# Two-layer graph and mixture kernel: layer 1's full pages in doubles of 512 rows of one expert

## The chip, the cores and the metric

The kernel runs on one core of a Trainium2 chip. The metric is the device time of one execution in microseconds; the time before is the median of three runs, 1977.85 us (1976.66 to 1979.0).

## What is computed

The input is 128 graphs of 64 nodes with 256 features, 8192 tokens in all. Two layers follow each other; each has a graph convolution over the 64 nodes and then a mixture of experts. The change concerns only the mixture of the second layer (layer 1), cut to what matters:

```python
x_flat = x.reshape(-1, D_MODEL)                       # 8192 x 256
gate_logits = x_flat @ Wg + bg + bias                 # 8 experts
topk_vals, topk_idx = jax.lax.top_k(gate_logits, 2)
topk_w = jax.nn.softmax(topk_vals, axis=-1)
h = relu(einsum('td,edh->teh', x_flat, W1) + b1)      # 256 -> 512, per expert
y = einsum('teh,ehd->ted', h, W2) + b2                # 512 -> 256
out = einsum('ted,te->td', y, combine)                # the two chosen experts, weighted
```

The input of this mixture is the layer's normalized x, and its result is added to x.

## The kernel before

The kernel computes each expert only for its own tokens. While layer 1's graph stage runs over 32 blocks of 256 tokens, a router (class `Router`, the object `r1`) sends each token's row of 258 words (256 features, the token's number, and the difference of its two logits) into a table in DRAM, at the next free place of the expert: L408, an indirect DMA from GpSimd, twice for a token. An expert's rows lie together. Afterwards the experts' rows are worked through in **pages** of 256 rows. A remainder of at most 128 rows is a half page.

How many pages each expert has is known only at run time. `page_table` (L432) computes on VectorE, in some fifty small instructions, a list of pages (row in the table, expert) and a list of half pages, into the tile `tab`; `load` (L547) reads four entries at a time into registers. The program holds a fixed number of page bodies: `likely` pages and half pages always run, and a block under `tc.If` (L1602) holds further ones, for routings that need more. With this kernel's numbers 58 full and 7 half pages always run, and the conditional block doesn't.

Four **first pages**, numbered -4 to -1, are the first 256 rows of experts 0 to 3. They are found full after block 16 (`look`, L179), and are fetched while the graph stage still runs (`fetch_first`, L568); their work is spread over the end of that stage and the transition from it.

One page goes through these steps, each a helper:

- `fetch1` (L1169) on SyncE's queue loads the page's rows into `px` (six buffers), and `load1` (L1162) the expert's first matrix with its bias into `pw` (three buffers) and the second bias into `pb2` (four).
- `flip1` (L1188): TensorE turns the rows (four instructions of L89), ScalarE copies them to `pxT`.
- `up` (L1195): the first product on TensorE (L1206), with relu on ScalarE (L1209).
- `down` (L1212): the second product (L1220), with the expert's matrix in `fw2`, which is resident.
- `share` (L1224): the weight of the expert, from the difference of logits.
- `answer` (L1234): on VectorE bias (L1237) and weight (L1239) into `py_s` (three buffers), and then, for each tile of 128 rows, `add` (L423).
- `add` (L425) is an indirect DMA from GpSimd that adds 128 rows of 256 words to the output in DRAM, at the tokens' rows, which it reads from `px`. A token appears in a page once, so the two adds of a page are declared independent; an add of another page waits until both have landed. A `px` buffer is free when its adds have landed.

`run` (L1593) lines pages up: at each step the page two ahead is fetched, the present page is turned, the former page finished (`share`, `down`, `answer`), and the present one goes `up`. The order is written out by hand: pages in order, with five of the seven half pages put in at every eighth page and the last two at the end (L1598 to L1601). The order on TensorE, VectorE and ScalarE is the program's own. SyncE and GpSimd's queues are put in order by a scheduler. [...]

At the transition the order is: `page_table`; `share` and `answer` of page -4; `flip1(-2)`; `down(-3)`; `up(-2)`; `share` and `answer` of page -3; and then `run`, whose first steps fetch page -1 and page 0, turn page -1, finish page -2, and take page -1 `up`.

Of the kernel before, what the change touches and what calls it, by code (L numbers as in the profile page):

```python
# [19 lines left out]
P = 128  # L20
# [86 lines left out]
class Router:  # L107
# [15 lines left out]
    def __init__(self, tc, pool, small, dram, n, D, E, K, T, pg, S, epoch, name, R, likely, halves, total=None, like=None):  # L123
        nc = tc.nc
        self.tc, self.nc, self.pool, self.small = tc, nc, pool, small
        self.n, self.D, self.E, self.K, self.T, self.pg, self.S, self.name = n, D, E, K, T, pg, S, name
        self.epoch, self.EP, self.pitch = epoch, epoch * T * P, S + pg
        self.halves = halves
        self.pages = K * n // pg + (E // 2 if halves else E - 1)
        self.likely_pages, self.likely_halves = likely  # L130
        self.full_pages = -(-(K * n - E * (pg - 1)) // pg)
        self.chunks = E + (K * (n - 3 * T * P) + E * self.EP) // S if S < n else E
        self.J = (n - 1) // S + 1
        self.spare = self.chunks * self.pitch
        self.W = D + 2
        assert T == 2 and epoch == 4 and n % self.EP == 0 and S % pg == 0 and (5 * T * P <= S or S >= n)
        assert self.pages <= 4 * P and self.spare + pg < 2 ** 24
        if like is None:
            self.tri = pool.tile([P, P], BF16, name=name + "tri")
            self.ones = pool.tile([P, P], BF16, name=name + "ones")  # L140
            make_upper_triangular(nc, self.tri, diag=False)
            nc.gpsimd.memset(self.ones, 1.0)
        else:
            self.tri, self.ones = like.tri, like.ones
        self.R = R
        self.seen = None
        self.expert = self.iota([P, E], [[1, E]], 0, "expert")
        self.page = self.iota([P, 4], [[1, 4]], 4, "page")
        self.total, self.each = total, (1 if total is not None else K)
        self.dest = self.iota([P, T, K], [[P * self.each, T], [0 if self.each == 1 else 1, K]], self.each, "dest")  # L150
        self.base = pool.tile([P, E], F32, name=name + "base")
        nc.vector.tensor_scalar(self.base, self.expert, float(self.pitch), None, op0=ALU.mult)
        self.zero = pool.tile([P, 3 * E], F32, name=name + "zero")
        nc.gpsimd.memset(self.zero, 0.0)
        self.map = pool.tile([P, self.J, E], F32, name=name + "map")
        nc.gpsimd.memset(self.map, 0.0)
        nc.vector.tensor_copy(self.map[:, 0, :], self.base)
        if self.J > 1:
            self.nth = self.iota([P, self.J, E], [[1, self.J], [0, E]], 0, "nth")
            self.end, self.delta, self.alloc, self.none = (  # L160
                pool.tile([P, E], F32, name=name + x) for x in ("endrow", "delta", "alloc", "none"))
            self.used = pool.tile([P, 1], F32, name=name + "used")
            for t, v in ((self.delta, 0), (self.alloc, 1), (self.used, E), (self.none, 1)):
                nc.gpsimd.memset(t, float(v))
            nc.vector.tensor_scalar(self.end, self.base, float(S), None, op0=ALU.add)
        self.filler = pool.tile([P, pg // P, self.W], F32, name=name + "filler")
        nc.gpsimd.memset(self.filler, 0.0)
        fill_to = self.filler[:, :, D].bitcast(I32)
        if total is None:
            self.answer = dram.tile([n * K, D], F32, name=name + "y")  # L170
            nc.gpsimd.iota(fill_to, pattern=[[0, pg // P]], base=n * K, channel_multiplier=0)
        else:
            nc.gpsimd.iota(fill_to, pattern=[[P, pg // P]], base=n, channel_multiplier=1)
            nc.sync.dma_start(out=total[n:n + pg, :].rearrange("(t p) d -> p t d", p=P), in_=self.filler[:, :, :D])
        self.table = dram.tile([self.spare + pg, self.W], F32, name=name + "x")
        self.taken = None
        self.fill(nc.sync, self.spare)

    def look(self, m):  # L179
# [10 lines left out]
        v.memset(self.firsts, 0.0)  # L190
        v.tensor_scalar(self.firsts[:, :m], t, float(self.spare), None, op0=ALU.add)
        self.full_pages -= m

    def look_back(self):

# [227 lines left out]
    def add(self, i, x, y):  # L423

        i, d = f"{self.name}add{i}", self.nc.gpsimd.indirect_dma_start(  # L425
            out=self.total[:, :],
            out_offset=bass.IndirectOffsetOnAxis(ap=x[:, self.D:self.D + 1].bitcast(I32), axis=0),
            in_=y, in_offset=None, compute_op=ALU.add)
        self.tc.declare_no_dep(d.ins, group=i, reason="a page has a token once")
        self.tc.add_to_no_dep_group(i, d.ins)  # L430

    def page_table(self, scratch):  # L432
# [94 lines left out]
        if self.halves:  # L527
# [8 lines left out]
            v.tensor_scalar(self.tab[:, 2, :], row, float(self.spare), None, op0=ALU.add)  # L536
            v.tensor_scalar(self.tab[:, 3, :], exp, float(E - 1), None, op0=ALU.min)

    def fill_end(self, e):

        if e % 4 == 0:
# [28 lines left out]
        d = self.nc.sync.dma_start(out=out, in_=self.table[ds(row, self.pg), :].rearrange("(t p) d -> p t d", p=P))  # L570
        self.tc.declare_no_dep(d.ins, group=self.name + "late", reason="full pages get no rows")

    def fetch_half(self, row, out):

        n = self.pg // 2
        self.nc.sync.dma_start(out=out, in_=self.table[ds(row, n), :].rearrange("(t p) d -> p t d", p=min(n, P)))

    def fetch(self, i, row, out):
        d = self.nc.sync.dma_start(out=out, in_=self.table[ds(row, self.pg), :].rearrange("(t p) d -> p t d", p=P))
        if i < self.full_pages:  # L580
            self.tc.declare_no_dep(d.ins, group=self.name + "fill", reason="full pages have no filler rows")
            self.tc.add_to_no_dep_group(self.name + "full", d.ins)
# [11 lines left out]
def two_layer_gnn_moe_kernel(ctx: ExitStack, tc: tile.TileContext, a: dict, out: bass.AP):  # L594
# [107 lines left out]
    with tc.tile_pool(name="c0", bufs=1) as c0, \  # L702
# [196 lines left out]
        for _ in norm_b(0):  # L899
# [3 lines left out]

        r0 = Router(tc, const, small, dram, N, D, E0, K0, T, P, 14 * P, 4, "r0", 3, ((K0 * N // P - EARLY) // 4 * 4 + 4, E0 // 2 - 4), True)
        r1 = Router(tc, const, small, dram, N, D, E1, 2, T, 2 * P, N, 4, "r1", 1,
                    (N // P - E1 // 4 - FIRST, E1 - 1), True, total=out, like=r0)
        assert W == r0.W
        r0.begin(counts, work, route)
        H, R, Q, V, S, Y = (chain(blocks, f) for f in (choose, residual_a, square_sum, normalize, slots, scale))
# [133 lines left out]
    with tc.tile_pool(name="wx0", bufs=3, reuse_waits="tile") as wx, \  # L1043
# [21 lines left out]
        def fetch(j):  # L1065
            Q = pairs[j]
            Q["px"] = px = wx.tile([P, 2, W], F32, name="px", bufs=22)
            if j >= npair:
                regs["row"] = r0.load(2, 4 * (j - npair), ENG.SP)
                for i in range(4):  # L1070
                    q, h = i // 2, i % 2 * P // 2
                    r0.fetch_half(regs["row"][i], px[h:h + P // 2, q:q + 1, :])
                return
            for q in range(Q["n"]):
                i = 2 * j + q
# [72 lines left out]
    fw2 = keep.tile([P, E1, KF, D], F32, name="fw2")  # L1148
    wx = ctx.enter_context(tc.tile_pool(name="wx1", bufs=2, side="right", reuse_waits="tile"))
    PG = 2 * P  # L1150
    pages = {i: dict(n=2 if i < r1.pages else 1) for i in range(-FIRST, r1.pages + E1)}
    regs = {}

    likely = r1.likely_pages
    some = r1.pages + r1.likely_halves

    def listed(i):

        what, i = (2, i - r1.pages) if i >= r1.pages else (0, i)
        return what, i, i % 4 == 0 or i == (r1.likely_halves if what else likely)  # L1160

    def load1(i, e):  # L1162
        Q = pages[i]
        Q["w"] = w = wx.tile([P, F1W], F32, name="pw", bufs=3)
        nc.sync.dma_start(out=w, in_=fw1[ds(e, 1)].rearrange("o p f -> p (o f)"))
        Q["b2"] = b2 = wx.tile([P, D], F32, name="pb2", bufs=4)
        nc.sync.dma_start(out=b2, in_=a["L1_ffn_b2"][ds(e, 1), :].to_broadcast([P, D]))

    def fetch1(i):  # L1169
        Q = pages[i]  # L1170
        Q["x"] = x = wx.tile([P, 2, W], F32, name="px", bufs=6)
        if i < 0:
            if i == -FIRST:
                regs["first"] = r1.load_first(0, ENG.SP)
            r1.fetch_first(regs["first"][i + FIRST], x)
            load1(i, i + FIRST)
            return
        what, m, new = listed(i)
        if new:
            regs["row", what], regs["esp", what] = r1.load(what, m, ENG.SP), r1.load(what + 1, m, ENG.SP)  # L1180
        if what:
            r1.fetch_half(regs["row", what][m % 4], x[:, :1, :])
        else:
            r1.fetch(i, regs["row", what][m % 4], x)
        load1(i, regs["esp", what][m % 4])


# [46 lines left out]
    def answer(i):  # L1234
# [2 lines left out]
        nc.vector.tensor_add(y[:, :n, :], Q["py"][:, :n, :], Q["b2"].unsqueeze(1).to_broadcast([P, n, D]))  # L1237
        for t in range(n):
            nc.vector.tensor_scalar(y[:, t, :], y[:, t, :], p[:, t:t + 1], None, op0=ALU.mult)  # L1239
            r1.add(i, Q["x"][:, t, :], y[:, t, :])  # L1240

    with tc.tile_pool(name="c3", bufs=1, reuse_waits="tile") as c3, \
            tc.tile_pool(name="work3", bufs=2, reuse_waits="tile") as work, \
# [309 lines left out]
            (3, place1),  # L1553
            (4, load_w2),
        ))
        r1.page_table(work.tile([P, 512], F32, name="scratch", bufs=1))
        share(-4)
        answer(-4)
        flip1(-2)
# [6 lines left out]
    with tc.tile_pool(name="pt4", bufs=2, space=PSUM, reuse_waits="tile") as pt_pool, \  # L1566
# [7 lines left out]
        def finish(i):  # L1574
            if i >= 0:
                what, m, new = listed(i)
                if what == 0 and m < E1:
                    r1.fill_end(m)
                if new:
                    regs["e", what] = r1.load(what + 1, m, ENG.PE)  # L1580
            share(i)
            down(i, regs["e", what][m % 4] if i >= 0 else i + FIRST)
# [12 lines left out]
            staggered(len(order), [(lag, lambda n, f=f: f(order[n]))  # L1595
                                   for lag, f in ((-2, fetch), (0, then(flip1)), (1, finish), (0, then(up)))])

        order = list(range(-2, likely))  # L1598
        for i in range(r1.pages, some - 2):
            order.insert(order.index(E1 * (i - r1.pages + 2)), i)  # L1600
        run((*order, *range(some - 2, some)))  # L1601
        with tc.If(r1.needed(likely)):  # L1602
            run((*range(likely, r1.pages), *range(some, r1.pages + E1)))


# [30 lines left out]
```

## Time and profile before

| What | Value |
|---|---|
| Median of three runs | 1977.85 us |
| The profiled execution | 1981.85 us, span 1979.7 us |
| TensorE busy | 1852.6 us, 94% of the span |
| VectorE, ScalarE, GpSimd busy | 58%, 51%, 57% |
| Granted TensorE clock, mean | 0.972 |
| Adds to the output (L425) | 131, 1553 ns each, 203.4 us |
| Loads of matrices (L1165) | 69, 514 KB each |
| Loads of rows of full pages (L579, L570) | 62, 258 KB each |

Times are of one execution recorded by the hardware profiler. A group of instructions is named by its line, engine, operation and tiles; "idle before" is the time its engine stood still just ahead of it, and what follows the arrow ended that wait. A view in order of time gives start and duration in us, and the wait in square brackets. PE is TensorE, DVE VectorE, ACT ScalarE, POOL GpSimd, and SPq the DMA queue of SyncE; a line there is the issue of a transfer and not the transfer itself. The experts' pages of layer 1 fill the stretch from about 1475 us to the end.

### The profile page before, as it was taken

To read this page: it belongs to the slowest core of one execution; us is meant where nothing else is said; L and a number is where in the kernel's file an instruction comes from. 1 tells how busy PE (TensorE), PEld (TensorE's weight loads), DVE (VectorE), ACT (ScalarE), POOL (GpSimd) and SP (SyncE) were. 2 spreads that over 40 slices of the span, in tenths; PEclk is the share of its full clock that TensorE was granted. 3 is DMA by queue.
4 is the path that set the end of the run, shared out by engine and by line. 5 is a ranking of instruction groups with operands and counts; after the bars stand their busy time and mean duration, and the time that the engine had idled before them with its cause. 6 is when DMAs were issued, how large, how long until landed. Compare 5 with 4: busy or idle time off the path is not lost. (4 is left out here: it accounts for less than half of the span.)

```text
span 1979.7 us, 35753 instructions
## 1 busy us (share of the span) xinstructions
PE 1852.6 (94%) x9906; PEld 1611.9 (81%) x9906; DVE 1150.0 (58%) x4248; ACT 1001.9 (51%) x2047; POOL 1134.9 (57%) x1113
## 2 busy tenths in 40 slices
PE   7999999999956898999989899999999999999992
PEld 6888888888845777888877788888888888888882
DVE  5899999999975333344333479999952222222221
ACT  5888888888831222222222266666643333333331
POOL 1377777777677677777777634444444434444433
PEclk9999999999977999999999899999999999999996
DMA  4234555553377988766665799787338766666663
GB/s 128 70 128 141 162 165 163 161 165 130 126 249 231 298 260 259 217 205 208 211 206 177 297 337 336 270 271 268 123 116 197 174 149 163 159 162 164 161 158 62
DMA packets 260780, 377.37 MB, mean 191 GB/s; under 512 B 54216, under 2 KB 214616, under 8 KB 260576
## 3 DMA queue, kind: packets, MB, share of 16 engines
q1 hardware_dynamic: 183600, 228.63, 38.8%
q0 software_dynamic: 62736, 135.21, 22.4%
q10 hardware_dynamic: 14240, 11.12, 1.7%
q8 instruction: 90, 1.47, 0.3%
q14 instruction: 114, 0.93, 0.2%
HBM read 211.67 MB, written 165.50 MB: 191 GB/s over the span
## 5 line engine op out<-in xcount | busy, mean ns | idle before, releaser
L408 POOL DMA_INDIRECT r0x<-xs,r0row x384 | 386.4, 1006 | 216.3 <-ACT lat L810 113.7
L415 POOL DMA_INDIRECT r0y<-px x390 | 378.9, 972 | 123.1 <-DMA r0y<-px 50.0
L1115 PE MATMUL py<-lat,pxT 128*128 x1616 | 386.4, 383 | 19.3 <-ACT pxT L1089 15.9
L425 POOL DMA_INDIRECT out_x<-py_s,px x131 | 203.4, 1553 | 294.1 <-DMA out_x<-py_s,px 189.3
L1119 DVE TENSOR_SCALAR px<-py,px 128x256 f32<-128x256 f32 x390 | 170.8, 480 | 306.2 <-PE py L1115 301.5
L1115 PEld LDWEIGHTS py<-lat,pxT 128*128 128x128 f32 x1616 | 293.1, 191 | 60.2 <-ACT pxT L1089 21.8
L1089 ACT COPY pxT<-pt 128x512 f32<-128x512 f32 x188 | 109.7, 585 | 346.1 <-PE pt L1086 232.3
L1209 ACT ACTIVATE phid<-ph,pw 128x256 f32<-128x256 f32 (+1 forms) x264 | 122.0, 462 | 294.6 <-issue 146.9
L408 POOL DMA_INDIRECT r1x<-xs,r1row x128 | 136.1, 1063 | 184.2 <-ACT hn L1349 54.7
L821 PE MATMUL ps<-lat 128*128 128x256 f32 x1024 | 238.9, 382 | 0.0
L785 PE MATMUL ph<-lat 128*128 128x256 f32 x1024 | 232.5, 386 | 2.7 <-DVE lat L808 2.0
L1220 PE MATMUL py<-fw,phid 128*128 (+1 forms) x1016 | 230.7, 380 | 1.8 <-issue 1.0
L1206 PE MATMUL ph<-pxT,pw 128*128 128x256 f32 (+1 forms) x1056 | 227.2, 368 | 0.6 <-DMA pw<-in_L_ffn_W1b 0.6
L785 PEld LDWEIGHTS ph<-lat 128*128 128x128 f32 x1024 | 195.4, 193 | 29.4 <-issue 2.4
L821 PEld LDWEIGHTS ps<-lat 128*128 128x128 f32 x1024 | 193.5, 192 | 27.9
L1206 PEld LDWEIGHTS ph<-pxT,pw 128*128 128x128 f32 x1056 | 192.8, 190 | 26.0 <-issue 1.4
L1237 DVE TENSOR_TENSOR py_s<-py,pb 128x512 f32<-128x512 f32 (+1 forms) x67 | 44.5, 664 | 290.7 <-DMA out_x<-py_s,px 232.7
L1220 PEld LDWEIGHTS py<-fw,phid 128*128 128x128 f32 x1016 | 187.9, 190 | 25.3 <-issue 1.6
L1086 PE MATMUL pt<-ident,px 128*128 128x128 f32 x780 | 120.7, 276 | 10.5 <-DMA px<-r0x 10.3
L1086 PEld LDWEIGHTS pt<-ident,px 128*128 128x128 f32 x780 | 97.3, 142 | 35.1 <-issue 7.0
L808 DVE SCALAR_TENSOR_TENSOR lat<-ph,c_L_gnn_b,rms 128x256 f32<-128x256 f32 x256 | 111.9, 476 | 22.9 <-ACT rms L72 22.9
L788 ACT ACTIVATE lat<-ph,c_L_gnn_b 128x256 f32<-128x256 f32 x256 | 103.5, 470 | 32.6 <-PE ph L785 28.3
(353 smaller groups left out, 2882.7 us busy)
## 6 DMA issues: line engine op xcount, KB each, us to landing
y<-r0y SPq DMA_DIRECT2D x64, 768.0 KB
px<-r0x SPq DMA_DIRECT2D x376, 129.0 KB
pw<-in_L_ffn_W1b SPq DMA_DIRECT2D x69, 514.0 KB
x<-x SPq DMA_DIRECT2D x64, 256.0 KB
px<-r1x SPq DMA_DIRECT2D x62, 258.0 KB
pb<-in_L_ffn_b SPq DMA_DIRECT2D x69, 128.0 KB
r0x<-r0filler ACTq DMA_DIRECT2D x64, 129.0 KB
lat<-in_x SPq DMA_DIRECT2D x32, 256.0 KB
```

Source lines behind the costliest of these rows:

```text
L408: i = self.nc.gpsimd.indirect_dma_start(out=self.table[:, :], out_offset=bass.IndirectOffsetOnAxis(ap=row[:, t, k:k + 1], axis=0), in_=xs[ ...
L415: d = self.nc.gpsimd.indirect_dma_start(out=self.answer[:, :], out_offset=bass.IndirectOffsetOnAxis(ap=x[:, self.D:self.D + 1].bitcast(I32 ...
L425: i, d = f"{self.name}add{i}", self.nc.gpsimd.indirect_dma_start(out=self.total[:, :], out_offset=bass.IndirectOffsetOnAxis(ap=x[:, self.D ...
L785: nc.tensor.matmul(ph[:, c, :], lhsT=w1[:, k, ts(2 * j + c, P)], rhs=B["aggT"][:, k, :], start=(k == 0), stop=(k == KD - 1))
L808: nc.vector.scalar_tensor_tensor(hT[:, c, :], B["ph", c // 2][:, c % 2, :], b1[:, c:c + 1], B["rms"], op0=ALU.add, op1=ALU.mult)
L821: nc.tensor.matmul(B["po"][:, t, :], lhsT=B["hT"][:, c, ts(t, P)], rhs=w2[:, c, :], start=False, stop=(t == T - 1 and c == KH - 1))
L1086: nc.tensor.transpose(pt[:, k, ts(q, P)], Q["px"][:, q, ts(k, P)], ident)
L1115: nc.tensor.matmul(py[:, q, :], lhsT=xT[q][:, k, ts(h, P)] if parts == 2 else xT[:, k, ts(q, P)], rhs=lat[:, ds(e, 1), k, :].rearrange("p ...
L1119: nc.vector.tensor_scalar(px[:, q, :D], py[:, q, :], px[:, q, D + 1:D + 2], None, op0=ALU.mult)
L1206: nc.tensor.matmul(ph[c - c0][:, :m], lhsT=w[:, k * F1 + c * P:k * F1 + (c + 1) * P], rhs=Q["xT"][:, k, :m], start=(k == 0), stop=(k == KD ...
L1209: nc.scalar.activation(hid[:, c, :m], ph[c - c0][:, :m], AF.Relu, bias=w[:, KD * F1 + c:KD * F1 + c + 1], scale=1.0)
L1220: nc.tensor.matmul(py[:, t, :], lhsT=Q["hid"][:, c, ts(t, P)], rhs=fw2[:, ds(e, 1), c, :].rearrange("p o d -> p (o d)"), start=(c == 0), s ...
```

## The change

Full pages of one expert are taken in twos, a **double** of 512 rows: one load of rows into `px4` (three buffers), one load of the matrix and the bias, and two pages that share them. The four adds of a double are in one group without waits between. What remains of an expert is at most one **single** (256 rows, or a remainder of over 128) and one half page. `page_lists` makes three lists in place of `page_table`'s two; 28 doubles, 2 singles and 7 halves always run. Halves and then singles are put in between doubles, the first ahead of page 16, then one every four pages; nothing follows the last double. `px` now has three buffers and serves first pages, singles and halves; `pb2` has three instead of four. A second stretch of zero rows is kept at the end of the table and of the output, for doubles that are empty; their token numbers are written by a small DMA in `look`.

```diff
         else:
             nc.gpsimd.iota(fill_to, pattern=[[P, pg // P]], base=n, channel_multiplier=1)
-            nc.sync.dma_start(out=total[n:n + pg, :].rearrange("(t p) d -> p t d", p=P), in_=self.filler[:, :, :D])
-        self.table = dram.tile([self.spare + pg, self.W], F32, name=name + "x")
+            for i in range(2):
+                nc.sync.dma_start(out=total[n + i * pg:n + (i + 1) * pg, :].rearrange("(t p) d -> p t d", p=P),
+                                  in_=self.filler[:, :, :D])
+        self.table = dram.tile([self.spare + (pg if total is None else 2 * pg), self.W], F32, name=name + "x")
...
         self.full_pages -= m
+        if self.total is not None:
+            nc, pg, more = self.nc, self.pg, self.pool.tile([P, self.pg // P], I32, name=self.name + "more")
+            nc.gpsimd.iota(more, pattern=[[P, pg // P]], base=self.n + pg, channel_multiplier=1)
+            self.fill(nc.sync, self.spare + pg)
+            with nc.allow_non_contiguous_dma(reason="a column"):
+                nc.sync.dma_start(out=self.table[self.spare + pg:self.spare + 2 * pg, self.D:self.D + 1].bitcast(I32)
+                                  .rearrange("(t p) d -> p (t d)", p=P), in_=more)
...
-        self.tc.declare_no_dep(d.ins, group=i, reason="a page has a token once")
+        self.tc.declare_no_dep(d.ins, group=i, reason="an expert has a token once")
         self.tc.add_to_no_dep_group(i, d.ins)
...
+    def page_lists(self, scratch):
...
+        v.tensor_sub(full, full, self.taken)
+        v.tensor_scalar(two, full, 0.5, 0.25, op0=ALU.mult, op1=ALU.subtract)
+        v.tensor_scalar(two, two, MAGIC, None, op0=ALU.add)
+        v.tensor_scalar(two, two, -MAGIC, None, op0=ALU.add)
+        v.tensor_scalar(big, left, pg / 2.0, None, op0=ALU.is_gt)
+        v.scalar_tensor_tensor(half, left, 0.0, big, op0=ALU.is_gt, op1=ALU.subtract)
+        v.scalar_tensor_tensor(one, two, -2.0, full, op0=ALU.mult, op1=ALU.add)
+        v.tensor_add(one, one, big)
...
+        for m, (num, step) in enumerate(((two, 2 * pg), (one, pg), (half, 0))):
...
+            v.tensor_tensor_scan(cum, num, self.zero[:, :E], 0.0, op0=ALU.add, op1=ALU.add)
+            v.tensor_tensor(le, wide(cum, 1), wide(self.page, 2), op=ALU.is_le)
+            v.tensor_reduce(exp, le, op=ALU.add, axis=AX.X)
...
+            v.tensor_scalar(self.tab[:, 2 * m, :], no, float(self.spare), None, op0=ALU.add)
+            v.tensor_scalar(self.tab[:, 2 * m + 1, :], exp, float(E - 1), None, op0=ALU.min)
...
-    def fetch(self, i, row, out):
-        d = self.nc.sync.dma_start(out=out, in_=self.table[ds(row, self.pg), :].rearrange("(t p) d -> p t d", p=P))
+    def fetch(self, i, row, out, n=None):
+        d = self.nc.sync.dma_start(out=out, in_=self.table[ds(row, n or self.pg), :].rearrange("(t p) d -> p t d", p=P))
...
-                    (N // P - E1 // 4 - FIRST, E1 - 1), True, total=out, like=r0)
+                    (N // P // 2 - E1 // 2, E1 // 4, E1 - 1), True, total=out, like=r0)
...
-        Q["b2"] = b2 = wx.tile([P, D], F32, name="pb2", bufs=4)
+        Q["b2"] = b2 = wx.tile([P, D], F32, name="pb2", bufs=3)
...
     def fetch1(i):
         Q = pages[i]
-        Q["x"] = x = wx.tile([P, 2, W], F32, name="px", bufs=6)
+        what, m, new = listed(i) if i >= 0 else (None, None, None)
+        if what == 0 and i % 2 == 1:
+            Q.update(x=pages[i - 1]["x4"][:, 2:, :], w=pages[i - 1]["w"], b2=pages[i - 1]["b2"])
+            return
+        if what == 0:
+            Q["x4"] = wx.tile([P, 4, W], F32, name="px4", bufs=3)
+            Q["x"] = Q["x4"][:, :2, :]
+        else:
+            Q["x"] = wx.tile([P, 2, W], F32, name="px", bufs=3)
...
-        if what:
-            r1.fetch_half(regs["row", what][m % 4], x[:, :1, :])
+        row = regs["row", what][m % 4]
+        if what == 0:
+            r1.fetch(2 * m, row, Q["x4"], 2 * PG)
         else:
-            r1.fetch(i, regs["row", what][m % 4], x)
+            r1.fetch_rows(row, Q["x"][:, :Q["n"], :], Q["n"] * P)
         load1(i, regs["esp", what][m % 4])
...
-            r1.add(i, Q["x"][:, t, :], y[:, t, :])
+            r1.add(i // 2 * 2 if 0 <= i < 2 * ND else i, Q["x"][:, t, :], y[:, t, :])
...
-        r1.page_table(work.tile([P, 512], F32, name="scratch", bufs=1))
+        r1.page_lists(work.tile([P, 512], F32, name="scratch", bufs=1))
...
-        order = list(range(-2, likely))
-        for i in range(r1.pages, some - 2):
-            order.insert(order.index(E1 * (i - r1.pages + 2)), i)
-        run((*order, *range(some - 2, some)))
-        with tc.If(r1.needed(likely)):
-            run((*range(likely, r1.pages), *range(some, r1.pages + E1)))
+        doubles, singles, halves = r1.likely
+        order = [*range(-2, 0), *span("double", 0, doubles)]
+        for n, i in enumerate((*span("half", 0, halves), *span("single", 0, singles))):
+            order.insert(order.index(2 * E1 + 4 * n), i)
+        run(order)
+        with tc.If(r1.needed(doubles)):
+            run((*span("double", doubles, ND), *span("single", singles, NS), *span("half", halves, NH)))
```

## The prediction

> **What bounds the kernel now.** I read the page first (busy shares, slices), then the two last stretches by engine, then the end and the start of the last stage instruction by instruction, on TensorE, GpSimd and SyncE.
>
> ```profile
> PE   7999999999956898999989899999999999999992
> ...
> L425 POOL DMA_INDIRECT out_x<-py_s,px x131 | 203.4, 1553 | 294.1 <-DMA out_x<-py_s,px 189.3
> ```
>
> ```profile
> 1475.00:1945.00 470.00, 464.74 (x2322) 409.10 (x2321) 112.47 (x330) 167.18 (x400) 192.53 (x124) 1.00 0.69 165
> 1945.00:1980.00 35.00, 0.43 (x2) 0.02 (x1) 1.78 (x6) 0.00 (x0) 10.88 (x7) 0.56 0.27 31
> ```
>
> Columns of the second view: stretch, length, busy us of TensorE, weight loads, VectorE, ScalarE, GpSimd, granted clock, DMA share, GB/s. From 1475 to 1945 the pages of layer 1 hold TensorE busy for 464.7 of 470 us. Then it is done, and 35 us pass with little but GpSimd's adds.
>
> ```profile
> 1933.28 3.62 PE L1220 MATMUL py<-fw,phid 128*128 x16
> ...
> 1943.46 1.97 PE L1220 MATMUL py<-fw,phid 128*128 x8 [0.82 <-DVE py_s L1237]
> ```
>
> ```profile
> 1949.63 1.56 POOL L425 DMA_INDIRECT out_x<-py_s,px  x1 [2.97 <-DVE py_s L1237]
> 1951.50 1.55 POOL L425 DMA_INDIRECT out_x<-py_s,px  x1 [0.30 <-issue]
> 1956.01 1.59 POOL L425 DMA_INDIRECT out_x<-py_s,px  x1 [2.97 <-DVE py_s L1237]
> 1957.90 1.55 POOL L425 DMA_INDIRECT out_x<-py_s,px  x1 [0.30 <-issue]
> 1962.58 1.55 POOL L425 DMA_INDIRECT out_x<-py_s,px  x1 [3.13 <-DMA out_x<-py_s,px]
> 1967.07 1.55 POOL L425 DMA_INDIRECT out_x<-py_s,px  x1 [2.94 <-issue]
> ```
>
> Counted back from the end, the pair at 1956.01 belongs to the page whose product (1933.28) ended at 1936.9: the adds run 19 us behind. A full page costs the add chain 1.55 + 0.30 + 1.55 and a wait of some 3.4 to 4.2 us for landing, 6.8 to 7.6 us. TensorE needs 7.34 us a page (1559.66 to 1567.00 in the timeline). So the chain is about as slow as TensorE, a little slower in places, and lags at the end. Rows (`px`) are refilled only after their adds have landed, so the lag eats the lead of the loads too:
>
> ```profile
> 1734.52 0.38 SPq L579 DMA_DIRECT2D px<-r1x  x1
> ...
> 1737.20 0.63 PE L89 MATMUL pt<-ident,px 128*128 128x128 f32 x4 [1.11 <-DMA px<-r1x]
> ```
>
> The load takes 2.7 us from issue to use, and TensorE stood 1.11 us. All gaps that the timeline gives TensorE from 1475 on are 1.11, 0.31, 0.64, 0.88, 0.44, 0.83, 0.24, 0.36 and 0.82: **5.6 us**.
>
> **What the skill says.** "DMA: Bandwidth & Descriptors", Rules for kernel authors: an accumulating DMA reads its destination and writes it later, so other accesses to the same bytes must wait for its semaphore. That is why adds of different experts wait, and why four adds of one expert, with different tokens, need not. The same page, Anatomy of one DMA, puts a fixed 2 us or so on a transfer issued by GpSimd, mostly the receipt of the last byte. The trace shows 2.9 us between an add's end and the next add where little else runs. "TensorE: Matmul & The Clock Gate", Part 1, says that an idle array falls to half clock and needs about 3.4 us of work to come back. This trace shows that after a pause of 2.4 us:
>
> ```profile
> 1444.37 1.89 PE L1206 MATMUL ps<-pxT,pw 128*128 128x256 f32 x8
> ...
> 1456.63 3.04 PE L1220 MATMUL pz<-fw,phid 128*128 128x256 f32 x8
> ```
>
> Eight matmuls took 3.04 us instead of 1.89.
>
> **The change, part by part.**
>
> *Work on TensorE.* Before: 4 first pages, 58 full, 7 half. After: 4 first, 28 doubles (56 pages), 2 singles, 7 halves. The same matmuls. The reference's own inputs give expert counts 2376, 1857, 1398, 1995, 1907, 1549, 3665, 1637. The new lists then hold exactly 28, 2 and 7, so the conditional block stays out, as before.
>
> *Adds without waits.* A double costs the chain 4 x 1.55 + 3 x 0.30 + about 4 = 11.1 us against 2 x 7.34 = 14.7 us of TensorE. Two doubles and a half page cost 2 x 11.1 + (1.55 + 3.8) = 27.6 us against 29.4 + 3.7 = 33.1 us. So the chain keeps up and the gaps go: **-5.6 us** (bounds 0 and -5.6).
>
> *The tail.* Afterwards the last page is the second of a double. From the end of its product to the end of its second add I count 0.04 + 0.69 + 0.04 + 0.31 + 0.05 + 1.55 + 0.30 + 1.55 = 4.5 us, which is how the third early page went (product to 1486.36; an add would follow VectorE's 1487.13 + 0.31). From the last add's end to the span's end are 1979.7 - 1968.6 = 11.1 us now; I keep them. Tail after: 15.6. Tail before: 1979.7 - 1945.4 = 34.3. **-18.7 us** (bounds -15.7, if four open adds land 3 us later, and -18.7).
>
> *Loads.* A double brings 516 KB of rows, 514 KB of matrices and a bias once, for two pages. The matrices' traffic halves. Their lead in the listing is one double, 14.7 us, and SyncE may run further ahead: with three row buffers of a double it waits for the adds of three doubles back, with three matrix buffers for TensorE about two doubles back. Row load 2.7 us for 258 KB, matrices at most 4.8 us (issued at 1792.84, used at 1797.68): even in series, under 11 us for a double. Cost 0, hidden under TensorE's previous double.
>
> *Fewer row buffers for the first pages.* `px` falls from 6 to 3 buffers, and there are four first pages. The fourth (page -1) takes the buffer of page -4, so its load waits for page -4's two adds to land. In the changed program's order the load stands with these waits on two of GpSimd's add semaphores, and before all loads of doubles. Before, it was issued at 1335.54:
>
> ```profile
> 1335.54 0.39 SPq L570 DMA_DIRECT2D px<-r1x  x1
> ...
> 1474.96 0.60 PE L89 MATMUL pt<-ident,px 128*128 128x128 f32 x4
> ```
>
> ```profile
> 1476.13 1.62 POOL L425 DMA_INDIRECT out_x<-py_s,px  x1 [5.05 <-DVE py_s L1239]
> 1478.05 1.58 POOL L425 DMA_INDIRECT out_x<-py_s,px  x1 [0.30 <-DVE p L1231]
> 1485.41 1.55 POOL L425 DMA_INDIRECT out_x<-py_s,px  x1 [5.78 <-DMA out_x<-py_s,px]
> ```
>
> TensorE turns these rows at 1474.96, ahead of the products of page -2 in its queue, so everything stands behind that turn. The adds of page -4 begin only at 1476.13, after the tables are made on VectorE: 53 instructions from 1465.54 to 1474.52, 0.169 us each. `page_lists` has 59: +1.0. So adds at 1477.15 and 1479.07, the second ending at 1480.65. Landing: SyncE issues a waiting load about 0.7 us before GpSimd's next add starts (1712.54 against 1713.27), so a usual gap of 3.6 gives the issue at 1483.55 (2.9 gives 1482.85, the 5.78 seen here, among four loads that will now stand behind, gives 1485.7). Plus 2.7: the turn at 1486.25. Stall 1486.25 - 1474.96 = **+11.3 us** (10.6 to 15.6, the upper end with a load of 4.8). After it TensorE runs cold: at 1456.63 to 1461.25 its starts fell 1.10 + 0.37 + about 0.2 us behind the warm ones: **+1.7 us** (0.1 to 2.5). During the stall the double's rows and matrices are issued within some 3 us, and are needed 7.5 and 11 us after the turn: no second stall.
>
> *Set-up.* One more fill of zeros and one of the output's spare rows on SyncE near the start, one iota on GpSimd, and midway a column of 256 words into the table. SyncE's queue waits there for earlier sends, and the next sends for it. Row sends have slack (GpSimd 37.3 busy of 80 us from 1320), and the loads behind are blocks ahead. I take 0 (bounds 0 and +2).
>
> Sum: -5.6 - 18.7 + 11.3 + 1.7 = **-11.3 us**. Span 1979.7 to 1968.4; the profiled execution took 1981.85 with what lies around the span, so 1970.6. The median shown, 1977.85, is 4.0 below that execution; the same step makes it **1966.6**.
>
> **The rivals.**
> 1. *No stall at the start* (adds or loads get ahead): -24.3, 1953.6. The four open adds speak for a gain of this size; the load's wait on the add semaphores speaks against. 0.08.
> 2. *Long ends*: stall 15.6, cold 2.5, tail only -15.7, gaps gone: -3.2, 1974.7, within what can be told from no change (0.2%, 4 us). The 5.78 us speaks for it, the emptier DMA against. 0.11.
> 3. *Slower: doubles come late.* At each double's first turn TensorE waits for one large load of 516 KB, queued behind the former double's matrices. At 1.1 us each, as the worst load here, 27 doubles cost 29.7: +18.4, 1996. It decides from 11.3 / 27 = 0.42 us a double. For it: every late piece of TensorE's stage hung on such loads. Against: leads of 14.7 us and half the matrix traffic. 0.06.
> 4. *The lists overflow.* If a count crosses a multiple of 128 rows, the conditional block runs 4 doubles, 14 singles and a half page: 22 x 7.34 + 3.7 = +165, 2131. The nearest count is 13 tokens off. 0.02.
>
> **How the numbers follow.** Forecast 0.73, rivals 0.08, 0.11, 0.06, 0.02. Of the forecast, nearly all lies between 1959 and 1973; to leave no more than two in ten out I reach to 1957 below and 1974 above, which takes in part of the first two rivals. Faster: 0.73 and 0.08 and a little of rival 2, 0.84. Same: 0.09. Slower: 0.07.
>
> **What would show it.** A TensorE gap of 10 to 16 us near 1475, ended by the DMA of `px`, with slow matmuls after it; groups of four adds 1.85 us apart with one wait each; no DMA-ended gaps of TensorE later; 16 us from the last matmul to the end. A gap at every double, or none at the start, would make it wrong.

## The result, and the profile after

| | before | after |
|---|---|---|
| Median | 1978.42 us (6 runs, 1976.66 to 1982.21) | 1969.38 us (6 runs, 1965.24 to 1971.1) |
| Ratio to before | | 0.9949, 95% interval 0.9934 to 0.9964 |
| Profiled execution, span | 1979.7 us | 1969.2 us |
| Read from HBM | 211.67 MB | 193.27 MB |

The changed kernel is faster by half a per cent, about 9 us. Ratios, here and below, leave out executions over 1.5% above the fastest of their kernel, so that a ratio can differ a little from the quotient of the two medians. Lines have moved: the adds are now L436, the products L1289 (up) and L1303 (down), VectorE's bias L1320 and weight L1322, the loads L644, L649 and L652 (rows), L1240 (matrix) and L1242 (second bias).

First the page's group of adds, which answers to the line of L425 shown of before:

```profile
L436 POOL DMA_INDIRECT out_x<-py_s,px x131 | 202.8, 1548 | 282.5 <-DVE py_s L1322 179.3
```

The adds are as many and as long. What they wait for has changed: most of their idle time was ended by a landing (189.3 us), and now by VectorE, which hands them their data (179.3 us). So the chain of adds now follows TensorE.

Second, the stretches by engine (columns as in the prediction):

```profile
1475.00:1500.00 25.00, 14.45 (x59) 12.08 (x59) 6.83 (x33) 5.04 (x13) 9.39 (x6) 0.73 0.64 161
1500.00:1940.00 440.00, 440.00 (x2211) 389.27 (x2210) 101.87 (x311) 158.36 (x379) 184.15 (x119) 1.00 0.60 127
1940.00:1970.00 30.00, 13.17 (x63) 11.25 (x62) 3.59 (x12) 4.44 (x11) 9.28 (x6) 0.78 0.24 29
```

From 1500 to 1940 TensorE has no gap at all. In the first 25 us it is busy for only 14.45, at a granted clock of 0.73. That is the pause which the change brings, in order of time on TensorE, GpSimd and SyncE:

```profile
1478.76 1.62 POOL L436 DMA_INDIRECT out_x<-py_s,px  x1 [6.09 <-DVE py_s L1322]
1480.68 1.58 POOL L436 DMA_INDIRECT out_x<-py_s,px  x1 [0.30 <-issue]
1484.59 0.39 SPq L644 DMA_DIRECT2D px<-r1x  x1
1485.23 1.55 POOL L436 DMA_INDIRECT out_x<-py_s,px  x1 [2.96 <-DMA out_x<-py_s,px]
...
1487.26 1.11 PE L89 MATMUL pt<-ident,px 128*128 128x128 f32 x4 [10.55 <-DMA px<-r1x]
1488.17 5.92 PE L1303 MATMUL py<-fw,phid 128*128 128x256 f32 x16
...
1493.92 3.62 PE L1289 MATMUL ph<-pxT,pw 128*128 128x256 f32 x16
```

Read it from the top: page -4's two adds; when they have landed, SyncE issues page -1's rows (1484.59); 2.67 us later TensorE turns them, after 10.55 us of standing still. The sixteen matmuls that follow take 5.92 us, where the same form at full clock takes 3.62. The granted clock was 0.50 from the turn (1487.26) until 1492.80.

And the end, GpSimd and TensorE:

```profile
1949.56 3.62 PE L1303 MATMUL py<-fw,phid 128*128 x16
...
1954.57 1.55 POOL L436 DMA_INDIRECT out_x<-py_s,px  x1 [3.51 <-DVE py_s L1322]
1956.42 1.55 POOL L436 DMA_INDIRECT out_x<-py_s,px  x1 [0.30 <-issue]
```

The last adds now belong to the page whose product has just ended (1953.18). The tail is 1969.2 - 1953.18 = 16.0 us, where before it was 34.3 us.

The sum of the two traces: from the first full product (page -1's up) to the last matmul's end, 1478.85 to 1945.43 before and 1493.92 to 1953.18 after, 466.6 against 459.3, **-7.3 us**; the tail **-18.3 us**; the pause **+10.6 us**; the cold clock **+2.8 us** (turn to that product 6.66 us against 3.89); all that lies ahead of the pause **+1.6 us** more, of which 1.5 was there already when the first matmul of layer 1's graph stage began (L1377 at 1127.4 before, L1460 at 1128.9 after). Together about -10.6, and the spans differ by 10.5.

### The profile page after: what moved, and what is told of

Read it like the earlier page. It is cut to its first block, busy times and chain, and to the rows that moved or that the text cites. A ratio compares the mean times of both kernels' runs of the same rounds, so it can differ in the third digit from the quotient of the medians.

```text
span 1969.2 us, 35306 instructions
## 1 busy us (share of the span) xinstructions
PE 1852.8 (94%) x9906; PEld 1613.4 (82%) x9906; DVE 1146.4 (58%) x4256; ACT 1002.0 (51%) x2047; POOL 1134.5 (58%) x1114
## 3 DMA queue, kind: packets, MB, share of 16 engines
HBM read 193.27 MB, written 166.03 MB: 182 GB/s over the span
## 5 line engine op out<-in xcount | busy, mean ns | idle before, releaser
L436 POOL DMA_INDIRECT out_x<-py_s,px x131 | 202.8, 1548 | 282.5 <-DVE py_s L1322 179.3
L1303 PE MATMUL py<-fw,phid 128*128 (+1 forms) x1016 | 232.7, 382 | 0.0
L1289 PE MATMUL ph<-pxT,pw 128*128 128x256 f32 (+1 forms) x1056 | 227.0, 368 | 0.0
L1289 PEld LDWEIGHTS ph<-pxT,pw 128*128 128x128 f32 x1056 | 193.0, 190 | 24.7
L1303 PEld LDWEIGHTS py<-fw,phid 128*128 128x128 f32 x1016 | 189.6, 192 | 23.5
L1314 DVE TENSOR_SCALAR p<-p 128x2 f32<-128x2 f32 (+1 forms) x69 | 12.2, 177 | 218.5 <-ACT p L1313 218.5
L1320 DVE TENSOR_TENSOR py_s<-py,pb 128x512 f32<-128x512 f32 (+1 forms) x67 | 44.5, 664 | 143.7 <-PE py L1303 141.4
```

The source lines that it names most:

```text
L1289: nc.tensor.matmul(ph[c - c0][:, :m], lhsT=w[:, k * F1 + c * P:k * F1 + (c + 1) * P], rhs=Q["xT"][:, k, :m], start=(k == 0), stop=(k == KD ...
L1303: nc.tensor.matmul(py[:, t, :], lhsT=Q["hid"][:, c, ts(t, P)], rhs=fw2[:, ds(e, 1), c, :].rearrange("p o d -> p (o d)"), start=(c == 0), s ...
```

## The experiments

Two theories on the gain stood against each other. *Theory A*: adds without waits remove both the tail and the gaps. *Rival B*: it is the loads, halved for the matrices, whose lighter traffic lets adds land sooner. A third reading, *rival C*, is that the order (nothing behind the last double) makes the tail. The pause at the start was a theory with a chain of causes to test: lists on VectorE, then adds, then landing, then load. Further letters in the recorded expectations hold for their own run alone.

In three of the four sessions layer 0 took some 30% longer for every kernel, before among them, while the pages of layer 1 ran as elsewhere; so ratios to the kernel before, run beside each, and the last stretch of a trace are compared, and absolute times only within a session.

| Run | Time us | Before beside it | Ratio, 95% interval |
|---|---|---|---|
| changed kernel again (a1) | 2293.97 | 2305.01 | 0.9952, 0.9932 to 0.9972 |
| four row buffers (e1) | 2283.06 | 2310.4 | 0.9863, 0.9769 to 0.9956 |
| the same (e1b) | 2278.03 | 2305.01 | 0.9877, 0.9844 to 0.991 |
| the same (e1c) | 2278.03 | 2309.37 | 0.985, 0.9798 to 0.9902 |
| waits between pages (e2) | 2326.04 | 2310.4 | 1.0053, 1.0016 to 1.0089 |
| the same (e2b) | 2335.63 | 2305.01 | 1.0122, 1.0089 to 1.0155 |
| loads per page (e3) | 2284.9 | 2310.4 | 0.9881, 0.9795 to 0.9966 |
| both (e4) | 2364.36 | 2310.4 | 1.0229, 1.0141 to 1.0317 |
| before, halves inside (e5) | 2303.01 | 2305.01 | 0.9987, 0.9955 to 1.0018 |
| page -4 ahead of the lists (e6) | 1963.63 | 1980.55 | 0.9915, 0.9896 to 0.9935 |
| before, eight row buffers (e9) | 2030.35 | 1980.55 | 1.0243, 1.022 to 1.0266 |
| and six of the bias (e10) | 2315.76 | 2309.37 | 1.0036, 1.0 to 1.0071 |

### The pause: a fourth row buffer

```diff
-            Q["x"] = wx.tile([P, 2, W], F32, name="px", bufs=3)
+            Q["x"] = wx.tile([P, 2, W], F32, name="px", bufs=4)
```

> The changed kernel with four px buffers in place of three, so that the fourth first page has rows of its own. Theory A (the pause near 1475 us is only the fourth first page waiting for the first one's rows): the 10.6 us pause and the 2.8 us of slow clock behind it go, and the time falls by 13 us against the changed kernel, to about 1956 us. Rival B (something else at the transition is late as well, say the first double's 516 KB or the adds of the first pages): a pause of 5 us or more comes back within the next three pages, and the time falls by less than 8 us.

> The changed kernel with four px buffers again. The first run of it showed no pause of TensorE at all in the pages. Theory A: 13 us below the changed kernel of this job, 0.988 of the kernel before. Rival B (the pause covered something that is now late): less than 8 us below it.

> The changed kernel again, to stand beside the next runs on the same chip, since the first four ran on one that took 17% longer for every kernel. As measured before: 0.995 of the kernel before, a 10.6 us pause near 1475 us, 16 us from the last matmul to the end.

The transition on TensorE in the second of these runs:

```profile
1786.69 0.60 PE L89 MATMUL pt<-ident,px 128*128 128x128 f32 x4
1787.13 3.62 PE L1303 MATMUL py<-fw,phid 128*128 128x256 f32 x16
1790.59 1.03 PE L1289 MATMUL ph<-pxT,pw 128*128 128x256 f32 x4
1792.61 2.86 PE L1289 MATMUL ph<-pxT,pw 128*128 128x256 f32 x12 [1.00 <-DVE py_s L1320]
1795.31 0.60 PE L89 MATMUL pt<-ident,px 128*128 128x128 f32 x4
```

and the same place in the changed kernel of the same session:

```profile
1803.38 1.11 PE L89 MATMUL pt<-ident,px 128*128 128x128 f32 x4 [12.10 <-DMA px<-r1x]
1804.29 5.30 PE L1303 MATMUL py<-fw,phid 128*128 128x256 f32 x16
```

With four buffers page -1 has one of its own. The pause of 12.1 us is gone, a single microsecond is left, the turn takes 0.60 us instead of 1.11, and the product 3.62 instead of 5.30. The way from the transition to the end is 12.8 us shorter; the medians of that session differ by 16 us. The tail stays 16.0 us. Both expectations came out for theory A. So the gain of the wait-free adds and the cost of the missing buffer are separate terms, and with the cost taken away this version beats the kernel before in each of three comparisons (by about 1.3%), and the changed kernel in the one session that has both.

### The pause: page -4 ahead of the lists

```diff
-        r1.page_lists(work.tile([P, 512], F32, name="scratch", bufs=1))
         share(-4)
         answer(-4)
+        r1.page_lists(work.tile([P, 512], F32, name="scratch", bufs=1))
```

> The changed kernel with the weights and the answer of page -4 ahead of the three lists on VectorE, so that its adds need not wait for the lists; still three px buffers. Theory A (the pause is the chain lists on VectorE, adds of page -4, their landing, the load of page -1's rows): the adds then follow GpSimd's last row sends, some 5.5 us earlier, the pause falls from 10.6 to about 5 us and the time by 5 to 7 us. Rival D (the lists are then too late and the first double's rows, or the landing itself, hold TensorE as long): pause or pauses of 9 us or more in all, time unchanged.

```profile
1470.71 1.64 POOL L436 DMA_INDIRECT out_x<-py_s,px  x1 [0.75 <-DVE py_s L1322]
1472.65 1.58 POOL L436 DMA_INDIRECT out_x<-py_s,px  x1 [0.30 <-DVE scratch L576]
...
1476.50 0.39 SPq L644 DMA_DIRECT2D px<-r1x  x1
...
1479.35 1.11 PE L89 MATMUL pt<-ident,px 128*128 128x128 f32 x4 [5.34 <-DMA px<-r1x]
```

The adds start 8 us earlier than in the changed kernel, the load is issued 8.1 us earlier, and the pause halves, from 10.55 to 5.34 us. It doesn't shrink by all 8 us, since in this run TensorE itself reached the turn 2.7 us sooner (1474.0 against 1476.7); against TensorE the adds moved by 5.3 us, and the pause by 5.2. The load comes 2.27 us after the end of the second add here, and 2.33 us in the changed kernel: the chain lists, adds, landing, load holds link by link. The time came out as theory A had it: a ratio of 0.9915, where the changed kernel stood at 0.9949 and 0.9952 in other sessions, some 7 us less.

### The gain: waits, loads, and both

The waits put back between the two pages of a double (first line pair; e2), matrix and bias loaded for each page again (second; e3), and both (e4):

```diff
-            r1.add(i // 2 * 2 if 0 <= i < 2 * ND else i, Q["x"][:, t, :], y[:, t, :])
+            r1.add(i, Q["x"][:, t, :], y[:, t, :])
...
-            Q.update(x=pages[i - 1]["x4"][:, 2:, :], w=pages[i - 1]["w"], b2=pages[i - 1]["b2"])
+            Q["x"] = pages[i - 1]["x4"][:, 2:, :]
+            load1(i, regs["esp", what][m % 4])
```

> The changed kernel, with the adds of a double's two pages again waiting for each other; loads and order stay. Theory A (the missing waits let the add chain keep up): a page costs the chain 1.55 + 0.30 + 1.55 + about 4.1 = 7.5 us against 7.34, the lag comes back over 56 pages, the tail grows by 8 to 18 us and gaps return: 1978 to 1990 us. Rival B (half the matrix traffic makes the adds land sooner, about 3.5 us, and that is enough): 6.9 us a page, no lag, within 3 us of the changed kernel's 1969.

> The changed kernel with waits between the adds of a double's pages again. Theory A (waits make the lag): tail of 24 us or more and gaps from px, 10 us or more above the changed kernel of this job. Rival B (less traffic is enough on a chip whose adds land in 3 to 4 us): within 4 us of it.

> The changed kernel, with matrix and bias loaded for each page again instead of once for a double; adds without waits stay. Theory A (waits matter): a double costs the chain about 11.2 us against 14.7 of TensorE whatever the traffic, so within 3 us of the changed kernel's 1969. Rival B (the traffic matters): the adds land later, the DMA share rises from 0.60 to about 0.69, and lag or late loads come back: 1975 us or more.

> Both at once: adds of a double's pages wait for each other, and matrix and bias are loaded for each page. Both theories expect the lag of the kernel before: tail of 25 us or more and gaps, with the pause at the start on top, 1982 to 1993 us. If it stays near 1969, neither the waits nor the traffic made the gain, and the order of pages did (short pages spread, none at the end).

With the loads per page (e3) nothing is lost: 0.9881 (the changed kernel stood at 0.9952 in another session), a single gap of TensorE (11.79 us, the pause), 465.3 us from the turn to the last matmul, which is what the changed kernel took in its own run of that kind, and a tail of 16 us. The traffic does come back (DMA share 0.72 in 430 us of pages, against 0.60 in the changed kernel of a1), and landings that an add waits for do come later: 5.57 us on average, in 21 waits, against 4.17 us in 9 in a1. But half the matrix traffic is worth nothing that can be measured here, as long as the adds of a double don't wait for each other. With the waits the whole gain is lost and more: 1.0053 (e2) and 1.0122 (e2b). The trace of e2b shows six new gaps of TensorE, 12.7 us in all, the largest

```profile
2274.57 1.09 PE L89 MATMUL pt<-ident,px 128*128 128x128 f32 x4 [5.40 <-DMA px<-r1x]
```

and a tail of 2319.0 - 2294.5 = 24.5 us. So rival B falls and theory A holds, but in size it was too small: 9 to 21 us were expected from the waits, and the medians of e2b and a1 differ by 42. In the session of e2 the ratio of 1.0053 against 0.9952 makes it some 23 us. The two profiled executions differ by 34.5 us in span, and 28.6 of these lie in the pages (8.7 in the tail, 1.4 in the pause, 18.5 between); the rest is ahead of them, in the part that the edit doesn't touch. One place that shows how waits can cost more among doubles than among pages, on GpSimd and SyncE in the same run:

```profile
2002.65 1.55 POOL L436 DMA_INDIRECT out_x<-py_s,px  x1 [3.07 <-DMA out_x<-py_s,px]
...
2008.45 0.38 SPq L652 DMA_DIRECT2D px<-r1x  x1
2009.07 0.33 SPq L1240 DMA_DIRECT2D pw<-in_L_ffn_W1b  x1
2009.10 1.55 POOL L436 DMA_INDIRECT out_x<-py_s,px  x1 [3.06 <-DVE py_s L1322]
...
2010.18 0.34 SPq L649 DMA_DIRECT2D px<-r1x  x1
...
2010.96 1.55 POOL L436 DMA_INDIRECT out_x<-py_s,px  x1 [0.31 <-issue]
2011.08 0.34 SPq L1240 DMA_DIRECT2D pw<-in_L_ffn_W1b  x1
...
2020.03 1.55 POOL L436 DMA_INDIRECT out_x<-py_s,px  x1 [7.53 <-DMA out_x<-py_s,px]
```

Ahead of 2002.65, with no load issued beside them, adds land in 3.07 us. At 2008.45 one landing lets SyncE go, and it sends a double's rows, a matrix, a short page's rows (L649) and another matrix within 3 us. The adds of 2009.10 and 2010.96 are issued among them, and the next must wait 7.53 us. How much of the loss such places make is not shown: the mean wait for a landing is 4.29 us in e2b, against 3.97 in e5, which has no doubles. With waits and loads per page together (e4) it is worst: 1.0229, 47.75 us of gaps on TensorE in 23 places (the pause of 12.22 among them), a tail of 30.4 us, and a mean wait for a landing of 4.86 us. So traffic does count, but only where adds wait. The waits alone bring the tail back only in part (24.5 us); with the loads per page it is nearly that of the kernel before (30.4 against 34.3).

### The gain: the order alone

The kernel before, with all seven half pages inside the list:

```diff
-        for i in range(r1.pages, some - 2):
-            order.insert(order.index(E1 * (i - r1.pages + 2)), i)
-        run((*order, *range(some - 2, some)))
+        for i in range(r1.pages, some):
+            order.insert(order.index(6 * (i - r1.pages) + 16), i)
+        run(order)
```

> The kernel before, with all seven half pages among the full ones (ahead of page 16 and then every sixth), none at the end. Theory A (the add chain is behind as a whole): the chain has the same work and ends at the same time, within 3 us of the kernel before, tail still over 28 us after the last matmul. Rival C (the two half pages at the end, 4.5 us of chain each for 3.7 us of TensorE, make the tail): 6 us or more below the kernel before.

0.9987, no difference, and a tail of 31.6 us. Rival C falls: with waits, full pages at the end lag as half pages did.

### Could the kernel before be helped by more row buffers?

```diff
-        Q["x"] = x = wx.tile([P, 2, W], F32, name="px", bufs=6)
+        Q["x"] = x = wx.tile([P, 2, W], F32, name="px", bufs=8)
```

> The kernel before with eight px buffers in place of six. Theory A (the add chain, not the loads, sets the end): TensorE's px gaps shrink or go, but the adds end when they did, the tail grows by what the gaps lose, and the time stays within 3 us of the kernel before. Rival E (the late loads are a cost of their own): 5 us or more below it.

Both theories missed: 50 us slower. What SyncE waited for between 1500 and 1900 us (columns: us in total, times, longest), first before, then with eight buffers:

```profile
SPq L579 <- DMA out_x<-py_s,px: 264.3, 54, 7.1
```

```profile
SPq L1167 <- DVE py_s L1237: 169.6, 30, 8.0
SPq L1165 <- ACT phid L1209: 118.7, 27, 5.6
```

Before, SyncE stands at the row load until adds have landed. With eight buffers it no longer stands there. It stands at the load of the second bias, until VectorE has added the bias of four pages back; and VectorE's add waits for `py_s`, which the landing frees. Now compare where the loads fall against the next add, first before, then with eight buffers:

```profile
1712.54 0.38 SPq L579 DMA_DIRECT2D px<-r1x  x1
1713.15 0.43 SPq L1165 DMA_DIRECT2D pw<-in_L_ffn_W1b  x1
1713.27 1.55 POOL L425 DMA_INDIRECT out_x<-py_s,px  x1 [3.64 <-DMA out_x<-py_s,px]
...
1720.78 1.55 POOL L425 DMA_INDIRECT out_x<-py_s,px  x1 [4.11 <-DMA out_x<-py_s,px]
```

```profile
1742.93 1.55 POOL L425 DMA_INDIRECT out_x<-py_s,px  x1 [5.00 <-DMA out_x<-py_s,px]
1743.00 0.33 SPq L1167 DMA_DIRECT2D pb<-in_L_ffn_b  x1
1743.58 0.38 SPq L579 DMA_DIRECT2D px<-r1x  x1
1744.19 0.33 SPq L1165 DMA_DIRECT2D pw<-in_L_ffn_W1b  x1
...
1752.60 1.55 POOL L425 DMA_INDIRECT out_x<-py_s,px  x1 [6.28 <-DMA out_x<-py_s,px]
...
1752.79 6.49 PE L1220 MATMUL py<-fw,phid 128*128 x16 [3.82 <-DVE py_s L1237]
```

The row load went out 0.73 us ahead of the next add, and the matrix 0.12 us ahead. Now the row load goes out 0.65 us behind it and the matrix 1.26 us behind, and in the lines shown the adds land after 5.0 to 6.3 us instead of 3.6 to 4.1. Over the whole trace the mean wait ended by a landing is 4.79 us (44 waits) against 3.94 (48). The chain of adds, which was as slow as TensorE, is now slower, and the last line shows TensorE paying: 3.82 us of standing and then matmuls at 6.49 us instead of 3.62, at a granted clock of 0.56. Among all its pages TensorE now stands 39.4 us in 25 places, 37.3 us of it until VectorE's L1237 has emptied a product, and nowhere until a load has come. So late loads are not what holds TensorE here; late adds are. To test this reading, the bias got six buffers, so that SyncE need not wait for VectorE:

```diff
-        Q["b2"] = b2 = wx.tile([P, D], F32, name="pb2", bufs=4)
+        Q["b2"] = b2 = wx.tile([P, D], F32, name="pb2", bufs=6)
```

> The kernel before with eight row buffers (bufs=8 of px) and six of the second bias (bufs=6 of pb2, before 4). With eight row buffers alone the run was 1.0243 times before. Its trace shows SyncE no longer held by the landing of adds at the row load (264.3 us in 54 waits before, none then) but at the load of the second bias, by VectorE's add of the bias L1237 (169.6 us in 30 waits): the row load, which in before was issued at the landing, 0.7 us ahead of the next add, is then issued 0.65 us behind that add's start, and adds land 5.0 to 6.3 us later instead of 3.6 to 4.3. Theory C: what costs the 50 us is this place of the loads against the adds: an add that has loads issued beside it lands late, and the next waits for it. With six buffers of the second bias SyncE no longer waits for VectorE; it is paced by the matrices' three buffers, so by TensorE's up, some 4 us ahead of that page's adds. Then the waits of SyncE at L1167 go (under 20 us in all between 1500 and 1900), the adds' waits for landings are back to a mean of 3.4 to 4.2 us, and the time is within 0.6% of before, possibly a little faster (ratio 0.993 to 1.006). Rival D: rows loaded further ahead cost by themselves, wherever they are issued (more transfers in flight): the mean wait stays at 4.6 us or more and the ratio at 1.015 or more.

Most of the loss is gone: 1.0036 (1.0 to 1.0071), some 8 us, against 1.0243, with the same eight row buffers. The one trace of this version is of an execution of 2341.78 us, 26 us above the median of its runs; in it the way from page -1's turn to the last matmul still takes 492.7 us, against 470.5 before and 517.8 with eight row buffers alone. SyncE's waits, in a stretch of 440 us of this run:

```profile
SPq L579 <- DMA out_x<-py_s,px: 191.6, 43, 6.0
SPq L1165 <- ACT phid L1209: 100.9, 39, 5.6
```

and the place of the row load is the old one, ahead of the add, while that of the matrix changes from page to page:

```profile
2016.08 0.38 SPq L579 DMA_DIRECT2D px<-r1x  x1
...
2016.81 1.55 POOL L425 DMA_INDIRECT out_x<-py_s,px  x1 [3.63 <-DMA out_x<-py_s,px]
...
2023.18 0.38 SPq L579 DMA_DIRECT2D px<-r1x  x1
2023.90 1.57 POOL L425 DMA_INDIRECT out_x<-py_s,px  x1 [3.69 <-DVE py_s L1237]
2024.95 0.33 SPq L1165 DMA_DIRECT2D pw<-in_L_ffn_W1b  x1
...
2032.23 1.55 POOL L425 DMA_INDIRECT out_x<-py_s,px  x1 [4.90 <-DMA out_x<-py_s,px]
```

Rival D, that rows loaded further ahead cost by themselves, falls. Of theory C the time and the missing wait for VectorE came out; one detail did not: I expected SyncE to be paced by TensorE, and it stands at the row load again, now for the adds of eight pages back. The mean wait for a landing was 4.16 us, at the upper edge of the 3.4 to 4.2 expected; and the eight buffers alone were measured in another session than this run.

That the place of the loads causes the late landings is shown as far as one edit moved the loads and the waits together. Which load it is, no run tested, and the traces speak for the matrix and against the rows. At 2023.90 the row load stands ahead of the add as before, the matrix 1.05 us behind it, and the landing takes 4.90 us. In the trace of eight row buffers alone, with the row load behind the first add in all of them, 6 landings with the matrix ahead of that add took 4.0 us on average, and 29 with the matrix 0.5 us or more behind it 5.24 us. Whether packets of a load stand ahead of those of the add in the DMA engines, or share them, the traces don't tell.

A third run of the changed kernel with four row buffers, in the session of the run above:

> The changed kernel with four row buffers instead of three (as in the runs before it of the same edit, at 0.986 and 0.988 of the kernel before on a chip whose layer 0 was slower). Here on another chip, for its time. Theory A: no pause of TensorE at the transition, 12.8 us less than the changed kernel, which stood at 0.995 of before: ratio 0.986 to 0.990, span to the last matmul with a tail of 16 us. Rival: the pause only moves to a later wait and the gain is under 5 us: ratio 0.992 or more.

Its ratio, 0.985, is in line with the two before.

## Why the prediction was right

The forecast, faster with a pause at the start that takes back part of the gain, came out in sign, in size and in its parts: 1966.6 us was forecast, and the median is 1969.38. The terms were off by up to 1.7 us in both directions, and these errors cancel in part; that the sum of the traces (-10.5 us) lies so close to the -11.3 forecast owes something to luck.

- *Adds without waits, gaps.* Predicted -5.6 us, found -7.3. All later gaps are gone. The 1.7 us beyond the listed gaps lie in the matmuls themselves, which I had not priced: the same 2303 of them held TensorE busy for 461.3 us before and 459.3 us after.
- *The tail.* Predicted -18.7, found -18.3; of the experiments, only those with waits lengthen it: to 24.5 us with waits alone, to 30.4 with the loads per page as well. Loads alone and the order alone do not change it much (16 and 31.6 us, each near its own kernel).
- *The pause.* Predicted +11.3, found +10.55. Its links: lists on VectorE +1.0 predicted, +1.04 found (from the first list instruction to the bias of page -4, 10.29 against 9.25 us; the trace of before has 51 instructions there and not 53, so that the step forecast from the count of 6 was really one of 8, and its size a little lucky); load 2.7 predicted, 2.67 found; from the second add's end to the load 2.9 predicted, 2.33 found. The edit of one buffer and the edit of one place in the order each moved it as that chain says.
- *Cold clock.* Predicted +1.7, found +2.8. This term was mis-sized: I took the fall from a pause of 2.4 us, after which the granted clock was 0.50 for 3.4 us (1457.4 to 1460.8 before); after the new pause it was 0.50 for 5.5 us of work. The length of the pause alone doesn't set it: after 12.10 us in a1 the loss was smaller, 2.15 us (turn to the next product 6.04 us against 3.89).
- *Loads.* Cost 0 predicted. No gap of TensorE in the changed kernel is ended by a double's load, so rival 3 did not come. That loads also bring no gain that can be measured was shown by e3.
- *Set-up.* Predicted 0. In the graph stage of layer 1 none was seen (from the first to the last start of its matmuls L1377, after L1460, 320.2 us in both). The 1.6 us by which all came later was there nearly whole before that stage; whether the fills near the start have a part in it is not shown, and it is within what the spans of one kernel differ by here (1963.4 to 1969.3 for the changed one).
- *Rival 2*, long ends, was wrong on the tail (16.0, not 18.6) and on the pause (10.55, not 15.6), but right that the cold clock costs over 1.7 us. Rival 1 is the version with four buffers and not this one. The lists did not overflow (rival 4).

What I had priced too low, in the expectations of the experiments, was not in this sum: how dear the removed waits would have been with loads in doubles.

## What to carry to other kernels

When a chain of waiting accumulations is just about as slow as the engine that feeds it, taking the waits out pays twice, in late gaps and at the end, in this case 7.3 and 18.3 us. Look then at every buffer count that the same change lowers, because a first use that lies far ahead of the steady state can hang on a landing. A buffer added for a queue of transfers doesn't only let it run ahead: here it moved SyncE's wait from the row load to another load of the same queue, and so changed what its transfers collide with; read what the queue waits for before and after.

## What the runs showed of the hardware that was not expected

- The landing of an accumulating add depends on what is issued beside it: 3.07 us with no load near, 3.6 to 4.1 us in lines with a row load sent 0.7 to 1.0 us and a matrix 0.1 to 0.4 us ahead, 5.0 to 6.3 us in lines with the rows sent 0.65 us and the matrix 1.26 us behind the add's start, 7.53 us among four large loads (the longest of that run 8.75).
- Two more row buffers made the kernel before 50 us slower, and two more buffers of a bias of 128 KB took most of it back.
- After a pause of 10.55 us the granted clock was 0.50 for 5.54 us of work, and the turn and the product behind it took 2.8 us longer; after one of 12.10 us the loss was 2.15 us, after one of 5.34 us 1.9 us (e6, 5.80 us against 3.89). The 5.54 us lie between one and two of the windows of about 3.4 us that the Trainium skill describes as free-running ("TensorE: Matmul & The Clock Gate", Part 1).
